# Graph attention with relation biases: a batch's loads in smaller pieces, each waiting for an instruction of its own

## The chip, the cores and the metric

The kernel runs on one core of a Trainium2 chip. The metric is the device time of one execution in microseconds. Before the change the median of three runs is 593.66 us (593.51 to 594.92).

## What is computed

For 16 batches of 512 nodes with 512 features: a linear layer over the node and a condition vector, two attentions (one for each direction of the adjacency) of 16 heads over the first 20 nodes as keys and values, a ReLU, and the residual. Cut to what matters (B = 16, N = 512, F = 512, 11 relation labels, H = 16 heads of 32):

```python
q_exp = where(row_zero[..., None], 0.0, q[:, None, :])
self_feat = concatenate([v, q_exp], -1) @ W_self.T + b_self
output = self_feat
for d in range(2):
    A = (adj if d == 0 else swapaxes(adj, 1, 2))[:, :, :20, :]
    bias = A @ w_bias + b_bias
    qh = self_feat @ Wq[d].T + bq[d];  kh = self_feat[:, :20] @ Wk[d].T + bk[d]
    aff = where(A.sum(-1) > 0, einsum(qh, kh) / sqrt(32), NEG) + bias
    w = softmax(aff, -1)
    output += einsum(w @ self_feat[:, :20], Wout[d]) + bout[d]
return v + relu(output)
```

`row_zero` marks nodes whose features sum to 0.

## The kernel before

**Setup.** The first 100 us or so load the weights, and work out for all batches what depends on the first 20 nodes alone: the keys folded with the query weights (`g_d` in DRAM, 1216 KB a batch), the biases of the scores (`cq_d`, 20 KB for each of four copies) and the values folded with the output weights, in blocks (`bd_d`, 128 KB a batch).

**The loop.** Then a loop runs over the 16 batches b, and within it over four tiles of 128 nodes, `nt` = 0 to 3. The order of the work is written out by hand: every engine runs its instructions in the order of the program text, and so does SyncE (SP), which issues nearly all DMA transfers. A transfer whose operand or whose `behind` instruction isn't done stops SP, and all later transfers with it.

Each tile does the scores (`scores`, 128 matmuls on TensorE into `ps_s`), adds biases and mask, subtracts the maximum (`weigh`, VectorE), takes the exponential (`expo`, ScalarE), sums and divides (`normal`: sum and reciprocal on VectorE, product on GpSimd) and transposes (`turn`, VectorE). It is a pipeline: a tile's `normal` and `turn` run in the next tile's stage, and the product with the values (`attend`, 48 matmuls, line 426) for batch b - 1 runs in stage `nt` = 2 of batch b, with `finish` (the sum with `self_feat` on VectorE, the ReLU on ScalarE), `residual` (GpSimd) and `store` behind it. Between them the stages make the next batch's `self_feat` on TensorE by a scheme with seven products instead of eight (`product`, `x_sum` on GpSimd, `partial` and `joined` on VectorE), its masks and label biases (`mask_mul` on ScalarE, `mask_count`, `mask_sum`, `mask_spread`, `full_add`), and the row sums (`row_sum` on ScalarE, `row_mask`).

**The loads of a batch**, in SP's order over one period, with their size and what each waits for (the `ins` argument of `load_...`, by way of `behind`):

- `nt` = 0: the features transposed, `load_x(b + 1)`, two halves of 512 KB, behind the exponential of the tile before and behind `partial`; `row_mask` writes 2 KB of flags; `load_adj(b + 1, 0)`, 440 KB, behind `mask_sum`
- `nt` = 1: `load_nz` (256 KB, the flags on all partitions) behind an exponential; `load_cq` (4 x 20 KB); `load_adj(b + 1, 1)`, 440 KB, behind `normal`
- `nt` = 2: the features by rows, `load_xn(b + 2, 0)` and `(b + 2, 1)`, 512 KB each, behind the first sum and the first ReLU of `finish`; `load_keys(b + 1)`, first half, 608 KB, behind an exponential
- `nt` = 3: two stores of the output, 256 KB each; the second half of the keys behind `mask_sum`; a third store; `load_values(b)` (`vd`, 4 x 32 KB, one buffer); the fourth store at the start of the next `nt` = 0

Buffers: three of `x` and of `adj`, two of `xn` and of the keys `g`, one of `vd`. `residual` puts its output on a list, and `store()` issues what is on it: at the start of each stage and once in `nt` = 3.

Of the kernel before, what the change touches and what calls it, by code (L numbers as in the profile page):

```python
# [18 lines left out]
def gat_kernel(  # L19
# [87 lines left out]
    def load_xn(b, h, ins=None):  # L107
        t = xns[b, h] = load.tile([P, 2, F], F32, tag="xn", name=f"xn{b}_{h}")
        behind(nc.sync.dma_start(t, xn[b].rearrange("(p j) f -> p j f", j=4)[:, 2 * h : 2 * h + 2]), ins)

    def load_adj(b, h, ins=None):
        t = adjs[b, h] = load.tile([P, 2, S * L], I32, tag="adj", name=f"adj{b}_{h}", bufs=3)
        a = adj[b, h * 2 * P : (h + 1) * 2 * P].rearrange("(t p) d m l -> p t (d m l)", p=P)
        behind(nc.sync.dma_start(t, a), ins)

    def load_cq(b):
        cqs[b] = load.tile([P, HL, S], F32, tag="cq", name=f"cq{b}")
        for a in range(HL):
            nc.sync.dma_start(
                cqs[b][bass.ts(a, R)].rearrange("p h m -> p (h m)"),  # L120
                cq_d[b : b + 1, bass.ts(a, HL)].rearrange("b h d m -> b (h d m)").partition_broadcast(R),
            )
# [9 lines left out]
    def load_values(b):  # L132

        vds[b] = gp.tile([P, HL, 2, DH], F32, tag="vd", name=f"vd{b}", bufs=1)
        for c in range(C):
            nc.sync.dma_start(
                vds[b][bass.ts(c, 32)].rearrange("p e i g -> p (e i g)"), bd_d[c, b].rearrange("r e i g -> r (e i g)")
            )
# [96 lines left out]
    def x_sum(b, n):  # L235

        t = sums[b, n] = xsum.tile([P, 2, HN], F32, tag=f"t{n}", name=f"t{b}_{n}")
        one, two = {
            1: lambda: (x_block(b, 0, 1), x_block(b, 0, 0)),
            2: lambda: (x_block(b, 1, 1), sums[b, 1]),  # L240
            3: lambda: (x_block(b, 1, 1), x_block(b, 0, 1)),
            4: lambda: (x_block(b, 1, 0), sums[b, 2]),
        }[n]()
        nc.gpsimd.tensor_sub(t, one, two)  # L244
# [49 lines left out]
    def joined(b, n, key, f, l):  # L294

        nc.vector.tensor_add(
            block(b, f, l), parts[b, key][:, : 2 * HN].rearrange("p (i n) -> p i n", i=2), us.pop((b, n))
        )
# [37 lines left out]
    def full_add(b, nt):  # L336
        f = fulls[b, nt] = msk.tile([P, H * S], F32, tag="full", name=f"full{b}_{nt}").rearrange(
            "p (g h m) -> p g h m", g=HL, m=S
        )
        shape = [P, HL, HL, S]  # L340
        nc.gpsimd.tensor_add(  # L341
            f, cqs[b].unsqueeze(1).to_broadcast(shape),
            adds[b, nt // 2][:, nt % 2].unsqueeze(2).to_broadcast(shape),
        )
# [19 lines left out]
    def weigh(b, nt, ps, between=None):  # L364
# [10 lines left out]
        nc.vector.tensor_sub(s, f, mx.unsqueeze(3).to_broadcast(full))  # L375
# [28 lines left out]
    def normal(b, nt, s):  # L404
        sm = soft.tile([P, 2, H], F32, tag="sm", name=f"sm{b}_{nt}")
        nc.vector.tensor_reduce(sm, s, AX.X, ALU.add)  # L406
        nc.vector.reciprocal(sm, sm)  # L407
# [24 lines left out]
    def finish(b, o, banks):  # L432

        for c in range(C):
            add = nc.vector.tensor_add(o[:, c], banks[c], sfs[b][:, c])  # L435
            if c == 0:
                done["add"] = add
        for c in range(C):
            relu = nc.scalar.activation(o[:, c], o[:, c], AF.Relu, bias=bo[:, c : c + 1])  # L439
            if c == 0:  # L440
                done["relu"] = relu
# [327 lines left out]
    with tc.manual_schedule():  # L769
# [11 lines left out]
        for b in range(B):  # L781
# [7 lines left out]
            for nt in range(NT):  # L789
# [22 lines left out]
                if nt == 0:  # L812
# [4 lines left out]
                    else:  # L817
# [6 lines left out]
                        if more:  # L824
                            load_x(b + 1, range(2), done["exp"])
                            load_x(b + 1, range(2, C), done["partial"])
# [21 lines left out]
                    if more:  # L848
                        x_sum(b + 1, 1)
                    else:  # L850
# [32 lines left out]
                if nt == 2:  # L883
# [4 lines left out]
                    if b > 0:  # L888
# [16 lines left out]
                    if b > 0 and more:  # L905
                        load_keys(b + 1, range(2), done["exp"])
                    if more:
                        full_add(b, NT - 1)
                    if b > 0:
                        for c in (0, 1):  # L910
                            residual(b - 1, c, o)

                if nt == 3 and more:
# [4 lines left out]
                    x_sum(b + 1, 4)  # L918
                    if b + 2 < B:
# [5 lines left out]
                    if b > 0:  # L925
                        load_keys(b + 1, range(2, C), done["masks"])
# [119 lines left out]
```

## Time and profile before

| | us |
|---|---|
| median of three runs | 593.66 |
| profiled execution, its time | 593.27 |
| its span, first to last instruction | 591.5 |
| TensorE (PE) busy with matmuls | 578.7 |
| VectorE (DVE) busy | 492.3 |
| ScalarE (ACT) busy | 395.6 |
| GpSimd (POOL) busy | 384.2 |
| mean DMA rate over the span | 210 GB/s |

A row of the costliest groups names the line, engine and operation, what is written from what, shapes and count; then busy time, mean duration in ns, and the idle time of the engine just before, with what ended it. PE is the matmul, PEld the loading of its weights, which overlaps it, SPq the queue of SyncE. "issue" stands for time in which an engine waited for nothing that the profile shows. In the list of DMA queues, q1 carries the transfers that the kernel issues from SyncE, and q8 and q14 are marked "instruction". A DMA row gives the size of one transfer and the time from its issue to its landing.

### The profile page before, as it was taken

The page shows a single profiled execution, that of the slowest core. Times are in us where ns is not written, and L with a number is a line of the kernel's source. Part 1 is how long each engine was busy: PE and PEld are TensorE (multiplying, and loading weights), DVE is VectorE, ACT ScalarE, POOL GpSimd, SP SyncE. Part 2 cuts the span into 40 slices and gives each one's busy share as a digit, 9 for nine tenths or more (in the row PEclk, how much of TensorE's full clock was granted, in tenths as well). Part 3 has the DMA queues.
Part 4 walks back from the last instruction along what each step waited for, and adds up shares of the span by engine and source line. Part 5 has one row for each costly group of instructions (what it writes and reads, how often), then busy time and mean ns, then how long its engine had stood idle before and what let it go on. Part 6 is the DMA issues. An engine that isn't in the chain of part 4 may idle for free.

```text
span 591.5 us, 30038 instructions
## 1 busy us (share of the span) xinstructions
PE 578.7 (98%) x13180; PEld 439.7 (74%) x13180; DVE 492.3 (83%) x785; ACT 395.6 (67%) x1162; POOL 384.2 (65%) x351
## 2 busy tenths in 40 slices
PE   8999999999999999999999999999999999999994
PEld 6654547888978687787878787788787878787882
DVE  0495565889898888999999999888989898989896
ACT  1234644587877677768686868677787877777661
POOL 2315663638677675758686777675858677776774
PEclk9999999999999999999999999999999999999997
DMA  8998999857848485767676766757585748582503
GB/s 294 385 406 299 332 376 329 257 126 199 223 154 229 155 236 148 206 168 209 184 208 163 223 173 202 171 181 208 164 217 170 216 149 232 158 238 85 167 13 142
DMA packets 98129, 124.10 MB, mean 210 GB/s; under 512 B 19952, under 2 KB 70160, under 8 KB 95952
## 3 DMA queue, kind: packets, MB, share of 16 engines
q1 hardware_dynamic: 96752, 120.31, 67.1%
q8 instruction: 103, 1.69, 1.2%
q0 software_dynamic: 672, 1.36, 1.0%
q10 hardware_dynamic: 576, 0.53, 0.3%
q14 instruction: 26, 0.21, 0.1%
HBM read 82.30 MB, written 40.24 MB: 207 GB/s over the span
## 4 chain that ended last, share of the span: by engine, by line
PE 94%; DVE 3%; DMA 1%; issue 1%; ACT 0%; POOL 0%; SPq 0%; DVEq 0%; POOLq 0%; ACTq 0%
PE ps_s L353 44%; PE ps_a L279 17%; PE ps_c L279 8%; PE ps_o L426 6%; PE ps_d L279 4%; PE ps_v L644 3%; PE ps_k L581 3%; PE ps_sf L202 2%; DMA ws_q<-in_wsT 1%; PE ps_kv L532 1%; DVE o L435 0%; PE ps_nz L186 0%; DVE wt L415 0%; DVE ps_s L371 0%; DVE sm L406 0%
## 5 line engine op out<-in xcount | busy, mean ns | idle before, releaser
L353 PEld LDWEIGHTS ps_s<-g,sf 128*32 128x32 f32 x8192 | 264.0, 110 | 19.8 <-issue 12.2
L353 PE MATMUL ps_s<-g,sf 128*32 128x152 f32 x8192 | 277.3, 293 | 0.5 <-ACT st L684 0.5
L334 ACT COPY both<-add 32x80 f32<-32x80 f32 x512 | 130.9, 256 | 54.8 <-DVE add L325 49.0
L408 POOL TENSOR_TENSOR s<-s,sm 128x640 f32<-128x640 f32 x63 | 80.3, 1275 | 98.0 <-DVE sm L407 98.0
L341 POOL TENSOR_TENSOR full<-cq,both 128x640 f32<-128x640 f32 x64 | 100.1, 1565 | 30.3 <-issue 24.3
L314 ACT ACTIVATE prod<-adj,wb_sb 128x80 f32<-128x80 int32 x330 | 112.5, 432 | 0.0
L380 ACT ACTIVATE s<-s 128x640 f32<-128x640 f32 x63 | 46.5, 738 | 69.4 <-DVE s L375 69.0
L444 POOL TENSOR_TENSOR o<-o,x 128x512 f32<-128x512 f32 x60 | 75.9, 1285 | 0.0
L367 DVE TENSOR_TENSOR full<-ps_s,full 128x608 f32<-128x608 f32 x63 | 49.1, 779 | 32.1 <-PE ps_s L353 26.6
L406 DVE TENSOR_REDUCE sm<-s 128x32 f32<-128x640 f32 x63 | 50.9, 808 | 8.8 <-ACT s L380 8.6
L279 PE MATMUL ps_a<-t,ws_s 128*32 128x246 f32 x960 | 55.5, 370 | 0.0
L371 DVE TENSOR_REDUCE ps_s<-full 128x32 f32<-128x640 f32 x63 | 52.2, 828 | 2.2
L415 DVE STREAM_TRANSPOSE wt<-s 128x640 f32<-128x640 f32 x63 | 52.8, 839 | 0.1
L375 DVE TENSOR_TENSOR s<-full,ps_s 128x640 f32<-128x640 f32 x63 | 51.6, 818 | 1.1
L426 PE MATMUL ps_o<-wt,vd 32*32 32x512 f32 (+5 forms) x816 | 40.8, 581 | 3.7 <-DVE wt L400 2.0
L279 PEld LDWEIGHTS ps_a<-t,ws_s 128*32 128x32 f32 x960 | 32.2, 110 | 15.5
L325 DVE TENSOR_REDUCE add<-prod 128x80 f32<-128x960 f32 x32 | 36.8, 1150 | 6.3 <-ACT prod L314 4.4
L244 POOL TENSOR_TENSOR t<-x 128x492 f32<-128x492 f32 x30 | 34.4, 1148 | 10.1 <-DVE full L367 5.2
L439 ACT ACTIVATE o<-o,bo 128x512 f32<-128x512 f32 x60 | 38.2, 708 | 0.6 <-POOL biased L881 0.6
L435 DVE TENSOR_TENSOR o<-ps_o,sf 128x512 f32<-128x512 f32 x60 | 36.8, 672 | 1.0 <-PE ps_o L426 1.0
L286 DVE SCALAR_TENSOR_TENSOR u<-nz,qw,ps_a 128x246 f32<-128x246 f32 x90 | 36.6, 449 | 0.0
L244 POOL TENSOR_TENSOR t<-x,t 128x492 f32<-128x492 f32 x30 | 34.4, 1147 | 1.2
(238 smaller groups left out, 722.7 us busy)
## 6 DMA issues: line engine op xcount, KB each, us to landing
g_d<-st SPq DMA_DIRECT2D x16, 1064.0 KB, 5.9
g<-g_d SPq DMA_DIRECT2D x28, 608.0 KB, 5.2
out_T<-o SPq DMA_DIRECT2D x60, 256.0 KB, 4.7
xn<-in_xn SPq DMA_DIRECT2D x28, 512.0 KB, 3.6
x<-in_xT SPq DMA_DIRECT2D x28, 512.0 KB, 4.3
adj<-in_adj SPq DMA_DIRECT2D x32, 440.0 KB, 5.0
nz<-nz_d SPq DMA_DIRECT2D x14, 256.0 KB, 4.0
wk<-in_wkT SPq DMA_DIRECT2D x2, 1024.0 KB, 8.0
```

The source lines that it names most:

```text
L244: nc.gpsimd.tensor_sub(t, one, two)
L279: nc.tensor.matmul(to, lhs, x[:, k], start=start, stop=stop, skip_group_check=n != 2)
L314: nc.scalar.activation(p[:, :, l], a[:, :, l], AF.Identity, scale=wb_sb[:, l : l + 1])
L334: nc.scalar.copy(adds[b, h][bass.ts(a, R), :, g], add[r].rearrange("p (t m) -> p t m", t=2))
L341: nc.gpsimd.tensor_add(f, cqs[b].unsqueeze(1).to_broadcast(shape), adds[b, nt // 2][:, nt % 2].unsqueeze(2).to_broadcast(shape),)
L353: nc.tensor.matmul(bank[bass.ts(a, R), bass.ts(j, WD // HL)], sfs[b][:, k, bass.ds(nt * P + (2 * g + j) * R, R)], keys[:, k, a], start=(k ...
L371: nc.vector.tensor_reduce(mx, f, AX.X, ALU.max)
L375: nc.vector.tensor_sub(s, f, mx.unsqueeze(3).to_broadcast(full))
L408: done["normal"] = nc.gpsimd.tensor_mul(s, s, sm.unsqueeze(3).to_broadcast(full))
L415: nc.vector.transpose(wts[b][:, nt], s.rearrange("p a h m -> p (a h m)"))
L426: nc.tensor.matmul(banks[a][bass.ds(at // 2 * DH, n * DH)].rearrange("p (t n) -> p t n", n=32), vd[r, bass.ds(at * DH, n * DH)], wt[r, :, ...
L444: nc.gpsimd.tensor_add(o[:, c], o[:, c], xs[b][:, c])
```

## The change

No compute instruction is added, removed or moved; each engine but SyncE keeps its order. On SyncE:

- `load_x`: four pieces of 256 KB instead of two of 512. Pieces 0 and 1 move into the end of `nt` = 3 of the batch before, after the stores, behind the subtraction of `weigh` and the exponential; pieces 2 and 3 go in `nt` = 0 behind the sum and the product of `normal`.
- `load_adj`: four pieces of 220 KB instead of two of 440. Each half's first piece waits as the half did; its second waits for an `x_sum`.
- `load_nz` waits for `weigh` instead of the exponential behind it, and `load_cq` for that exponential.
- `load_xn`: four pieces of 256 KB, behind an `x_sum` in `nt` = 1, the second and fourth sum of `finish`, and the sum of `normal`.
- `load_keys`: four pieces of 304 KB, behind `normal` and `full_add` in `nt` = 2, `x_sum` and `normal` in `nt` = 3.
- `load_values` of batch b - 1 moves from the end of `nt` = 3 of batch b - 1's period into `nt` = 0 of the next, after `row_mask` and ahead of `load_adj`, behind `joined`.
- Each output is stored right after its own `residual`.
- The first batches (b = 0, in part 1) keep their whole loads where there is no earlier stage to put them in.

SyncE's program grows from some 22 to some 30 transfers a period.

```diff
-    def load_adj(b, h, ins=None):
-        t = adjs[b, h] = load.tile([P, 2, S * L], I32, tag="adj", name=f"adj{b}_{h}", bufs=3)
+    def load_adj(b, h, ins=None, ts=slice(0, 2)):
+        if ts.start == 0:
+            adjs[b, h] = load.tile([P, 2, S * L], I32, tag="adj", name=f"adj{b}_{h}", bufs=3)
         a = adj[b, h * 2 * P : (h + 1) * 2 * P].rearrange("(t p) d m l -> p t (d m l)", p=P)
-        behind(nc.sync.dma_start(t, a), ins)
+        behind(nc.sync.dma_start(adjs[b, h][:, ts], a[:, ts]), ins)
...
                         if more:
-                            load_x(b + 1, range(2), done["exp"])
-                            load_x(b + 1, range(2, C), done["partial"])
+                            load_x(b + 1, range(2, 3), done["sum"])
+                            load_x(b + 1, range(3, C), done["normal"])
...
                         product(b, 3)
+                        if b > 1:
+                            load_values(b - 1, done["joined"])
                         mask_sum(b, 1)
                         if more:
-                            load_adj(b + 1, 0, done["masks"])
+                            load_adj(b + 1, 0, done["masks"], slice(0, 1))
...
                     if more:
                         x_sum(b + 1, 1)
+                        if b > 0:
+                            load_adj(b + 1, 0, done["xsum"], slice(1, 2))
...
                     if b > 0 and more:
-                        load_nz(b + 1, done["exp"])
-                        load_cq(b + 1)
+                        load_nz(b + 1, done["weigh"])
+                        load_cq(b + 1, done["exp"])
                     normal(*prev)
                     if b > 0 and more:
-                        load_adj(b + 1, 1, done["normal"])
+                        load_adj(b + 1, 1, done["normal"], slice(0, 1))
...
                         x_sum(b + 1, 2)
+                        if b > 0:
+                            load_adj(b + 1, 1, done["xsum"], slice(1, 2))
                         x_sum(b + 1, 3)
+                        if 0 < b < B - 2:
+                            load_xn(b + 2, 0, done["xsum"], slice(0, 1))
...
                         if b + 2 < B:
-                            load_xn(b + 2, 0, done["add"])
-                            load_xn(b + 2, 1, done["relu"])
+                            load_xn(b + 2, 0, done["add", 1], slice(1, 2))
+                            load_xn(b + 2, 1, done["add", 3], slice(0, 1))
                     normal(*prev)
+                    if 0 < b < B - 2:
+                        load_xn(b + 2, 1, done["sum"], slice(1, 2))
+                    if b > 0 and more:
+                        load_keys(b + 1, range(1), done["normal"])
...
                     turn(*prev)
-                    if b > 0 and more:
-                        load_keys(b + 1, range(2), done["exp"])
                     if more:
                         full_add(b, NT - 1)
+                        if b > 0:
+                            load_keys(b + 1, range(1, 2), done["full"])
                     if b > 0:
                         for c in (0, 1):
                             residual(b - 1, c, o)
+                            store()
...
                     x_sum(b + 1, 4)
+                    if b > 0:
+                        load_keys(b + 1, range(2, 3), done["xsum"])
...
                     if b > 0:
-                        load_keys(b + 1, range(2, C), done["masks"])
+                        load_keys(b + 1, range(3, C), done["normal"])
...
                     if b > 0:
-                        residual(b - 1, 2, o)
-                        store()
-                        load_values(b)
-                        residual(b - 1, 3, o)
+                        for c in (2, 3):
+                            residual(b - 1, c, o)
+                            store()
+                    if b + 2 < B:
+                        load_x(b + 2, range(1), done["weigh"])
+                        load_x(b + 2, range(1, 2), done["exp"])
```

More of the change, by code (lines that the diff above doesn't have):

```diff
@@ L243, in x_sum @@
         }[n]()
-        nc.gpsimd.tensor_sub(t, one, two)
+        done["xsum"] = nc.gpsimd.tensor_sub(t, one, two)
     def product(b, n):
@@ L294, in joined @@
     def joined(b, n, key, f, l):
-        nc.vector.tensor_add(
+        done["joined"] = nc.vector.tensor_add(
             block(b, f, l), parts[b, key][:, : 2 * HN].rearrange("p (i n) -> p i n", i=2), us.pop((b, n))
@@ L340, in full_add @@
         shape = [P, HL, HL, S]
-        nc.gpsimd.tensor_add(
+        done["full"] = nc.gpsimd.tensor_add(
             f, cqs[b].unsqueeze(1).to_broadcast(shape),
@@ L374, in weigh @@
         s = soft.tile(full, F32, tag="s", name=f"s{b}_{nt}", bufs=3)
-        nc.vector.tensor_sub(s, f, mx.unsqueeze(3).to_broadcast(full))
+        done["weigh"] = nc.vector.tensor_sub(s, f, mx.unsqueeze(3).to_broadcast(full))
         return s
@@ L406, in normal @@
         nc.vector.tensor_reduce(sm, s, AX.X, ALU.add)
-        nc.vector.reciprocal(sm, sm)
+        done["sum"] = nc.vector.reciprocal(sm, sm)
         done["normal"] = nc.gpsimd.tensor_mul(s, s, sm.unsqueeze(3).to_broadcast(full))
```

28 lines of the change are left out of this document (13 added, 15 removed).

## The prediction

> **What bounds the kernel now.** I read the page first: busy shares, the chain that ended last, the DMA queues.
>
> ```profile
> span 591.5 us, 30038 instructions
> PE 578.7 (98%) x13180; PEld 439.7 (74%) x13180; DVE 492.3 (83%) x785; ACT 395.6 (67%) x1162; POOL 384.2 (65%) x351
> q8 instruction: 103, 1.69, 1.2%
> PE 94%; DVE 3%; DMA 1%; issue 1%; ACT 0%; POOL 0%; SPq 0%; DVEq 0%; POOLq 0%; ACTq 0%
> L353 PE MATMUL ps_s<-g,sf 128*32 128x152 f32 x8192 | 277.3, 293 | 0.5 <-ACT st L684 0.5
> ```
>
> TensorE is busy for 98% and is 94% of the chain. The change touches loads and stores alone, so it can only win what TensorE loses, and the question is where that is. The kernel repeats one period per batch; its clearest mark is the attention product (L426, 48 matmuls). Busy time by stretch, from one such mark to the next (columns: length, busy time of PE, PEld, DVE, ACT, POOL, granted clock, DMA share, GB/s; the first row is all 14 periods):
>
> ```profile
> 133.53:566.24 432.71, 431.31 (x10981) 342.15 (x10977) 391.06 (x602) 327.33 (x985) 308.17 (x267) 1.00 0.66 185
> 164.05:194.95 30.90, 30.90 (x788) 24.38 (x785) 28.01 (x43) 23.50 (x71) 22.13 (x20) 1.00 0.66 191
> 194.95:226.85 31.90, 31.51 (x789) 24.34 (x785) 28.12 (x43) 23.50 (x71) 22.05 (x20) 1.00 0.65 184
> 226.85:258.90 32.05, 31.59 (x785) 24.41 (x785) 28.14 (x43) 23.46 (x71) 21.91 (x20) 1.00 0.64 181
> 258.90:289.38 30.48, 30.48 (x789) 24.15 (x785) 27.83 (x43) 23.53 (x71) 21.87 (x20) 1.00 0.69 193
> 381.01:413.01 32.00, 31.45 (x789) 24.28 (x785) 28.13 (x43) 23.50 (x71) 22.12 (x20) 1.00 0.65 184
> 413.01:444.15 31.14, 31.14 (x788) 24.31 (x784) 28.01 (x43) 23.50 (x71) 21.99 (x20) 1.00 0.69 189
> ```
>
> A clean period is 30.48 us at full clock. Fourteen would be 426.72; they take 432.71, so 5.99 us are lost in all. The five long ones lose 0.42, 1.42, 1.57, 1.52 and 0.66, together 5.59. What happens there shows in the order of time of the weight loads, two bad attention products whole, a good one, and the first row of two more bad ones:
>
> ```profile
> 194.95 0.21 PEld L426 LDWEIGHTS ps_o<-wt,vd 32*32 32x32 f32 x25 [0.24 <-issue]
> 196.45 0.15 PEld L426 LDWEIGHTS ps_o<-wt,vd 32*32 32x32 f32 x7 [1.29 <-issue]
> 226.84 0.14 PEld L426 LDWEIGHTS ps_o<-wt,vd 32*32 32x32 f32 x5 [0.24 <-issue]
> 228.36 0.34 PEld L426 LDWEIGHTS ps_o<-wt,vd 32*32 32x32 f32 x27 [1.38 <-issue]
> 258.90 0.25 PEld L426 LDWEIGHTS ps_o<-wt,vd 32*32 32x32 f32 x32 [0.24 <-issue]
> 381.01 0.21 PEld L426 LDWEIGHTS ps_o<-wt,vd 32*32 32x32 f32 x27 [0.24 <-issue]
> 413.00 0.15 PEld L426 LDWEIGHTS ps_o<-wt,vd 32*32 32x32 f32 x6 [0.24 <-issue]
> ```
>
> The stall comes after 25, 5, 27 or 6 loads, and where its end is shown it ends on "issue": no semaphore that the profile shows. So neither data nor a buffer is late. The instructions themselves are: q8 has 103 packets of 1.69 MB, 16 KB each, and 26,360 matmuls and weight loads by 103 are 256, so one packet brings 256 instructions of TensorE. These packets run on the same DMA engines as the data. Here is the DMA view of the stretches just before and just after 193.9, with the issue of the adj load among them:
>
> ```profile
> GB/s 351 334 334 304 253 235 202 201 137 71 17 90 103 45 45 77 103 33 31 77 74 32 1 14 0 0 0 72 187 216 330 330 345 330 460 302 244 144 101 72
> q1 hardware_dynamic: 584, 0.77, 69.7%
> issues: line engine op xcount, KB each, median us to landing
> adj<-in_adj SPq DMA_DIRECT2D x1, 440.0 KB, 5.1
> ...
> q8 instruction: 1, 0.02, 5.1%
> ...
> L114 SPq DMA_DIRECT2D adj<-in_adj x1: 368/368/368, 189.4 to 189.4; - x1
> ```
>
> From 189.0 to 193.9 there is no q8 row; in 193.9 to 195.1 there is one. The adj load (440 KB) was issued at 189.4 and landed 5.1 later, at 194.5: the instruction packet got its turn only when that load was draining, at 193.9 or just after, and TensorE went on at 196.45, 2.55 later. The load is slow at first (in slices of 0.12 us, some 100 GB/s or less from 190.1 to 192.4), then runs at 330. So the loss is this: **a block of instructions, asked for while a large load stands ahead of it in the DMA engines, comes too late.** At 128 score matmuls in 4.33 us (277.3 x 128 / 8192), a block lasts some 4 us, so it is asked for about that long before it is needed; that, and that it waits for everything issued before it, is my reading and not a row.
>
> The Trainium skill ("Runtime: NRT & Kernel Launch", Instruction fetch mechanics) says that engines refill in 16 KiB blocks of 256 instructions, and that crossing a block is mostly hidden. By that rule there is nothing to win, which is the first rival below; the trace agrees on the block (256), and in the five long periods not on the hiding (1.29 and 1.38 idle).
>
> **The change part by part.** No compute instruction is added, removed or moved. What changes is SP's queue. I lay it over one clean period whose attention product starts at 319.85, with the ends of the instructions that the new loads wait for.
>
> ```profile
> 307.47 0.88 SPq L136 DMA_DIRECT2D vd<-bd_d  x2
> 309.54 2.30 SPq L105 DMA_DIRECT2D x<-in_xT  x2
> 309.81 4.32 PE L353 MATMUL ps_s<-g,sf 128*32 128x152 f32 x128
> 310.90 1.28 POOL L408 TENSOR_TENSOR s<-s,sm 128x640 f32<-128x640 f32 x1 [0.45 <-DVE sm L407]
> 312.32 0.66 DVE L296 TENSOR_TENSOR sf<-ps_c,u 128x492 f32<-128x492 f32 x1
> 314.45 0.37 SPq L114 DMA_DIRECT2D adj<-in_adj  x1
> 314.65 1.05 POOL L244 TENSOR_TENSOR t<-x 128x492 f32<-128x492 f32 x1
> 319.85 2.24 PE L426 MATMUL ps_o<-wt,vd 32*32 32x512 f32 x48
> 323.93 4.10 SPq L109 DMA_DIRECT2D xn<-in_xn  x2
> 326.45 0.35 DVE L407 RECIPROCAL sm<-sm 128x32 f32<-128x32 f32 x1
> 334.08 1.28 POOL L408 TENSOR_TENSOR s<-s,sm 128x640 f32<-128x640 f32 x1
> 334.95 0.38 SPq L130 DMA_DIRECT2D g<-g_d  x1
> ```
>
> *The adj pieces, the term that counts.* The four vd loads now stand ahead of adj: they wait for the join (L296) that ends at 312.98 and take 0.44 each, to 314.8. So the first half (220 KB) issues at 314.8, 5.05 before the attention product, where 440 KB went at 5.40 before; the second half waits for the x sum that ends at 315.70, 4.15 before. A block that is needed early in the attention product was asked for early. In the periods lost to a stall after five or six loads (1.57 and 0.66) I take it as asked for before 5.05 ahead, so it now stands behind x and vd alone and is in time: 2.2 won. In the other three (1.42, 1.52, 0.42) it stands behind the first half: 220 KB less at 330 GB/s is 0.67 sooner, the issue is 0.35 later, so 0.3 each, 0.9 won. Sum 3.1. The bounds: all 5.99 won if no block comes late any more; nothing won if the second half is ahead of it too; worse than nothing under the second rival.
>
> *The other loads*, for their effect on blocks: x goes in four pieces where 1 MB went in two loads, keys in four of 304 KB, xn in four of 256 KB, so that what stands ahead of a block is about half. Outside the long periods only 5.99 - 5.59 = 0.40 is lost; I count nothing for it.
>
> *Data that might now be late.* x pieces 3 and 4 wait for the sum and the normalisation, the latter ending at 312.18, 0.3 after the issuing of today's second load is over (311.84); the x sum and the product that read them come after 319.85. The last keys piece waits for the normalisation that ends at 335.36, 0.4 after today's 334.95; the second half of the next scores reads it at 309.81 + 30.48 + 2.1 = 342.4, 7 us on. The last xn piece goes at 326.80, before the end of issuing today (328.03). All cost nothing.
>
> *vd* is moved furthest: from before 308.4 to 312.98, the last of four issuing at 314.3, behind the last store, all of x and nz_d; TensorE reads it at 319.85. All landings of vd in the steady periods (least, median, most), with its issue times in ns in the row above:
>
> ```profile
> L136 SPq DMA_DIRECT2D vd<-bd_d x56: 380/419/1392, 150.7 to 554.3; - x56
> ...
> DMA to landing us min/median/max: 2.6/4.0/5.5
> ```
>
> At the median the last lands at 318.3, at the most at 319.8, just in time. Only the longest issue (1.39, 1.0 more) and the longest landing together would make TensorE wait, 0.9 in such a period; in all 14 it would be 13, in one or two 1 to 2. I take 0, by the median. *SP* issues about 8 more transfers a period at 0.4, 3 us. It is in order, so behind each wait stand all later loads: behind vd's wait for the join stand adj, nz and cq, read only by the next stage on ACT, DVE and POOL, after 319.85. The instructions waited for end in the order of the queue, so no wait adds to another. *Stores* follow their own residual; no engine waits for a store.
>
> Sum against the profiled run: 593.27 - 3.1 = 590.2. The median of the three runs is 593.66, 0.4 higher; I go to **590.6**.
>
> **The rivals.** (1) *The packet waits as long as before*: both halves and nz are ahead of it, or the 5.6 us are lost to whichever load is ahead. For: the halves go 0.9 apart, and a slow start stays slow. Against: two of the five losses belong to early requests. Between 0 and 1.7 won: 592 to 594, say 593.4. The Trainium skill ("DMA: Bandwidth & Descriptors", Queues, rings and completion order) would have it here: engines take turns between queues packet by packet, so a backlog on q1 would hardly delay q8 and cutting it up would win nothing; that the packet came only as adj drained speaks against. (2) *Slower: the second half of adj has a slow start of its own.* Its place is 4.15 ahead of the attention product. The first half drains 193.9 - 189.4 - 0.67 = 3.8 after issue, 1.25 ahead; another 2.3 slow and 0.67 of data end 1.7 after the start, and TensorE goes on 2.55 later, at 4.3 instead of 1.5 (196.45 for 194.95). Three such periods lose 2.8 more, 8.4, less the 2.2 won: 599.5. It decides from about 1 us of slow start (3 x 1.0 against 3.1 won). Against it: today's second adj load, just behind the first in memory, landed so:
>
> ```profile
> DMA to landing us min/median/max: 3.5/3.5/3.5
> ```
>
> (issued at 195.9), 1.6 less than the first, so about 0.7 of a slow start at the most. (3) *More won*: every late block gone, 587.7.
>
> **How the numbers follow.** A difference under 0.3%, 1.8 us, cannot be told from none here. Forecast 0.53 (588.5 to 591.8), more won 0.06, rival 1 0.23, rival 2 and lesser delays of its kind 0.18 (595.5 to 600). Faster 0.59, same 0.23, slower 0.18. The range 588.0 to 596.0 holds the forecast, rival 1 and the mild part of rival 2; the forecast's own is 588.5 to 591.8.
>
> **What would show it.** Right: periods of 30.5 between attention products with at most two or three over 31, the "issue" idle before L426 in the middle of the product mostly gone, adj landings of 220 KB about 3 to 4 us, vd landed before each product. Wrong: as many periods near 32 as before (rival 1); an adj second half that lands over 4.5 us after issue and stalls above 2 us (rival 2); PE waiting for DMA vd at L426; DVE or POOL waiting for x, g or adj.

## The result, and the profile after

The changed kernel takes 588.80 us (median of six runs, 587.81 to 589.27), the kernel before 593.59 (six runs, 591.39 to 595.43): the ratio is 0.9909, 95% interval 0.9886 to 0.9931. So it is faster by about 0.9%, 4.8 us, in the direction of the forecast, and its median is 1.8 us under the forecast 590.6. On another chip the same two kernels later gave 588.08 and 591.40, ratio 0.9945 (0.9917 to 0.9974).

The profiled execution took 589.14 us, with a span of 587.3. From its page come busy times, the shares of the chain, the group of the scores and the queue of instruction packets.

```profile
span 587.3 us, 30302 instructions
PE 575.0 (98%) x13180; PEld 436.8 (74%) x13180; DVE 491.2 (84%) x785; ACT 395.5 (67%) x1162; POOL 384.3 (65%) x351
q8 instruction: 104, 1.70, 1.2%
PE 94%; DVE 3%; DMA 1%; issue 1%; ACT 0%; POOL 0%; SPq 0%; DVEq 0%; POOLq 0%; ACTq 0%
L356 PE MATMUL ps_s<-g,sf 128*32 128x152 f32 x8192 | 276.7, 293 | 0.5 <-ACT st L683 0.5
```

The page alone tells little: TensorE does the same 13,180 matmuls at the same price and is the bound as before. The difference is in the stretches, from one attention product (now L429) to the next. The first row is again all 14 periods; then come the three longest and, from 286.08, a clean one.

```profile
132.06:561.14 429.08, 428.51 (x10981) 339.57 (x10977) 390.38 (x602) 327.23 (x985) 308.25 (x267) 1.00 0.65 188
132.06:163.50 31.44, 30.87 (x789) 24.29 (x785) 28.01 (x43) 23.74 (x71) 22.94 (x21) 1.00 0.74 216
193.97:224.90 30.93, 30.93 (x789) 24.51 (x785) 28.00 (x43) 23.51 (x71) 22.10 (x20) 1.00 0.67 192
286.08:316.55 30.47, 30.47 (x788) 24.21 (x785) 27.84 (x43) 23.50 (x71) 22.03 (x20) 1.00 0.66 186
377.50:408.76 31.26, 31.26 (x788) 24.44 (x785) 28.01 (x43) 23.50 (x71) 22.17 (x20) 1.00 0.65 192
```

The clean period is unchanged (30.47), the 14 take 429.08 where they took 432.71: 3.63 of the 4.13 us between the two profiled executions (593.27 and 589.14). Of the rest, 1.47 lies ahead of the first product (it begins at 133.53 and 132.06; over all runs here between 132.06 and 136.73), and 0.97 goes the other way after the last. No period is near 32 any more. The weight loads of the worst product that is left, in order of time:

```profile
377.50 0.15 PEld L429 LDWEIGHTS ps_o<-wt,vd 32*32 32x32 f32 x6 [0.24 <-issue]
378.14 0.43 PEld L429 LDWEIGHTS ps_o<-wt,vd 32*32 32x32 f32 x26 [0.49 <-issue]
379.41 0.23 PEld L429 LDWEIGHTS ps_o<-wt,vd 32*64 32x64 f32 x16 [0.84 <-issue]
```

One stall of 0.49 after six loads stands where before had 1.29, 1.38 and their like, and it is not of their kind: here TensorE waits for data. Its product is made in groups of 32 partitions, and each of the four `vd` loads brings one group. These are SP's issues ahead of this product, the landings of the four `vd` loads, and a wait that TensorE's sequencer, which issues its instructions, has in this product:

```profile
370.27 1.35 SPq L174 DMA_DIRECT2D nz_d<-nz  x1
371.73 1.76 SPq L139 DMA_DIRECT2D vd<-bd_d  x4
...
DMA to landing us min/median/max: 3.8/3.9/5.0
...
L429 PEldq EVENT_SEMAPHORE  x1: 51/51/51, 378.1 to 378.1; - x1
```

The fourth `vd` load was issued at 373.07 and took 5.0: it landed at 378.03, 0.53 after the product had begun. The sequencer's wait for its semaphore ended at 378.11, and the next weight load started at 378.14. The row says "issue" because the wait stands on an instruction of the sequencer. In the product at 193.97 the third and fourth `vd` load landed 0.04 and 0.22 after its begin, and the load of weights that needs the fourth started 0.30 later than in a clean product. In both periods the issue of `nz_d` ahead of `vd` took 1.35 or 1.44 us, where the clean period from 286.08 has 0.38. A block of instructions was late in the product at 377.50 as well: after 27 loads there is another pause of 0.17, so without the wait for `vd` not all of the time would have been won.

The view of waits sums the idle time for the loads of weights between 140 and 565 us. First the kernel before, then the changed one (columns: what waited for what, us in total, times, longest):

```profile
PEld ps_o L426 <- issue: 19.0, 31, 1.5
PEld ps_s L353 <- issue: 10.6, 13, 0.8
```
```profile
PEld ps_o L429 <- issue: 15.6, 29, 0.8
PEld ps_s L356 <- issue: 11.4, 14, 0.8
PEld ps_c L282 <- issue: 1.0, 1, 1.0
```

Each product has two regular waits, 0.24 ahead of its first load and 0.84 ahead of its last 16 (both in the rows above), 1.08 in all. The stretch holds 13 products of the kernel before (the next begins at 566.24) and 14 of the changed one, so 14.0 and 15.1 us are the floor. Above it stood 5.0 us in five waits before, and now 0.5 in one, the wait for `vd`. The row of `ps_c` is the long period 132.06:163.50: a new stall in the stage work, not in a product.

The smaller loads land sooner. The DMA issues of the page (count, KB each, median us to landing), before and after:

```profile
g<-g_d SPq DMA_DIRECT2D x28, 608.0 KB, 5.2
...
x<-in_xT SPq DMA_DIRECT2D x28, 512.0 KB, 4.3
adj<-in_adj SPq DMA_DIRECT2D x32, 440.0 KB, 5.0
```
```profile
g<-g_d SPq DMA_DIRECT2D x56, 304.0 KB, 3.6
...
x<-in_xT SPq DMA_DIRECT2D x56, 256.0 KB, 3.3
...
adj<-in_adj SPq DMA_DIRECT2D x56, 220.0 KB, 3.3
```

So far most looks as forecast, but for the waits for `vd`. That the stalls went because adj was halved is, however, only a reading yet.

### The profile page after: what moved, and what is told of

Its sections match the earlier page's. It is cut to its first block, busy times and chain, and to the rows that moved or that the text cites. A ratio compares the mean times of both kernels' runs of the same rounds, so it can differ in the third digit from the quotient of the medians.

```text
span 587.3 us, 30302 instructions
## 1 busy us (share of the span) xinstructions
PE 575.0 (98%) x13180; PEld 436.8 (74%) x13180; DVE 491.2 (84%) x785; ACT 395.5 (67%) x1162; POOL 384.3 (65%) x351
## 4 chain that ended last, share of the span: by engine, by line
PE 94%; DVE 3%; DMA 1%; issue 1%; ACT 0%; POOL 0%; SPq 0%; DVEq 0%; POOLq 0%; ACTq 0%
PE ps_s L356 44%; PE ps_a L282 17%; PE ps_c L282 9%; PE ps_o L429 6%; PE ps_d L282 4%; PE ps_v L643 3%; PE ps_k L580 3%; PE ps_sf L205 2%; DMA ws_q<-in_wsT 1%; PE ps_kv L531 1%; DVE o L438 0%; PE ps_nz L189 0%; DVE wt L418 0%; DVE ps_s L374 0%; DVE sm L409 0%
## 5 line engine op out<-in xcount | busy, mean ns | idle before, releaser
L429 PE MATMUL ps_o<-wt,vd 32*32 32x512 f32 (+5 forms) x816 | 37.8, 578 | 2.3 <-DVE wt L403 2.0
```

Of the source, the lines that this page charges most:

```text
L429: nc.tensor.matmul(banks[a][bass.ds(at // 2 * DH, n * DH)].rearrange("p (t n) -> p t n", n=32), vd[r, bass.ds(at * DH, n * DH)], wt[r, :, ...
```

## The experiments

Each kernel stands beside the kernel before on the same chip. Times are medians; "lost" is the length of the 14 periods of the profiled execution less the clean 426.66 (14 x 30.476).

| kernel | us | before, same chip | ratio (95%) | 14 periods | lost |
|---|---|---|---|---|---|
| before (first profile) | 593.59 | | | 432.71 | 6.0 |
| changed kernel | 588.80 | 593.59 | 0.9909 (0.9886 to 0.9931) | 429.08 | 2.4 |
| adj in pieces only | 592.14 | 592.86 | 0.9991 (0.9961 to 1.0021) | 430.14 | 3.5 |
| changed, adj whole | 587.30 | 592.86 | 0.9905 (0.9886 to 0.9925) | 428.02 | 1.4 |
| changed, vd at its old place | 589.54 | 592.86 | 0.9943 (0.9923 to 0.9964) | 427.87 | 1.2 |
| before, 16 more matmuls at the start | 594.49 (one run) | 592.86 | | 431.42 | 4.8 |
| pieces on the old waits | 590.25 | 592.60 | 0.9961 (0.9945 to 0.9977) | 430.89 | 4.2 |
| x only | 591.20 | 592.60 | 0.9979 (0.9966 to 0.9992) | 430.64 | 4.0 |
| vd only | 590.45 | 592.60 | 0.9967 (0.9949 to 0.9984) | 430.04 | 3.4 |
| first adj load moved away | 590.11 | 592.60 | 0.9976 (0.9956 to 0.9995) | 430.82 | 4.2 |
| vd and x | 590.73 | 591.40 | 0.9985 (0.9963 to 1.0006) | 431.51 | 4.9 |
| changed, adj whole, a spare load | 588.07 | 591.40 | 0.9943 (0.9922 to 0.9964) | 427.14 | 0.5 |
| changed, adj whole, again | 587.73 | 591.40 | 0.9928 (0.9903 to 0.9953) | 426.76 | 0.1 |
| changed kernel, again | 588.08 | 591.40 | 0.9945 (0.9917 to 0.9974) | 426.88 | 0.2 |

One profile is one execution, and the kernel before alone spreads over 589.8 to 596.5 us; so the medians decide on time, and a profile only on where a loss lies. The kernel before was profiled once, on the first chip; what its loop loses on the other chips is not known.

**Is it the blocks of instructions?** Eight more warming matmuls in the setup, with nothing else touched. Each counts as two, so 16 weight loads and 16 matmuls more are in TensorE's stream, and every 256th instruction falls 16 loads earlier in the loop.

```diff
-            for _ in range(7):
+            for _ in range(15):
                 nc.tensor.matmul(warm[:, :P], ones, ones, start=True, stop=True)
```

> The kernel before, with 8 more warm-up matmuls on TensorE ahead of the first load's landing: 16 more pairs of weight load and matmul, 32 instructions, so every block of 256 begins 16 pairs earlier in each later stage. Theory: the stalls in the attention products that came after 25, 27, 5 and 6 weight loads come after 9 and 11, and in the other two batches they leave the product (they would fall 11 and 10 pairs ahead of it, into the scores). Rival (a data or buffer wait): they stay after 25, 27, 5 and 6. Time within 1 us of before either way.

The weight loads of two products in order of time:

```profile
198.44 0.15 PEld L426 LDWEIGHTS ps_o<-wt,vd 32*32 32x32 f32 x9 [0.24 <-issue]
199.57 0.21 PEld L426 LDWEIGHTS ps_o<-wt,vd 32*32 32x32 f32 x23 [0.97 <-issue]
...
382.61 0.16 PEld L426 LDWEIGHTS ps_o<-wt,vd 32*32 32x32 f32 x11 [0.24 <-issue]
384.00 0.20 PEld L426 LDWEIGHTS ps_o<-wt,vd 32*32 32x32 f32 x21 [1.24 <-issue]
```

Where the stalls of these two batches stood after 25 and 27 loads, they now stand after 9 and 11: earlier by 16, exactly the loads that were added. In two more products the place fits too: a stall of 0.68 after 30 loads where before had 0.26 after 46, and, as expected, none where before had one after 5 and after 6. The time, 594.49, is 1.6 above the median of before, not within 1, but it is a single run, and before itself reached 596.5 on this chip. No data and no buffer moved, so the stall belongs to a place in the stream of instructions. This step is shown.

The packet records of the kernel before tell what TensorE waits for there. In all five products with a stall it goes on 1.4 to 1.5 us after the end of a packet of q8 (these start at 163.28, 194.00, 225.97, 380.21 and 411.43). The five packets took 0.88 to 0.98 us, the median of all being 0.97. So they ran no slower than others, they began late.

**Was it adj in pieces?** First adj in four pieces alone, all else as before:

```diff
-                            load_adj(b + 1, 0, done["masks"])
+                            load_adj(b + 1, 0, done["masks"], slice(0, 1))
...
+                        if b > 0:
+                            load_adj(b + 1, 0, done["xsum"], slice(1, 2))
...
-                        load_adj(b + 1, 1, done["normal"])
+                        load_adj(b + 1, 1, done["normal"], slice(0, 1))
...
+                        if b > 0:
+                            load_adj(b + 1, 1, done["xsum"], slice(1, 2))
```

> The kernel before, with adj alone cut into four pieces of 220 KB; all other loads as before. Theory of the prediction (a block of instructions waits for the adj load ahead of it): a block asked for after the first half and before the second waits 0.67 us less, in all five long periods, so 2.5 to 3.3 us are won: 590 to 591. Rival (all loads' backlog counts, adj is only one of them): under 1.5 us won, 592 to 593.5.

The stalls stay at their places and are shorter (rows of the second part of three products):

```profile
194.55 0.15 PEld L427 LDWEIGHTS ps_o<-wt,vd 32*32 32x32 f32 x7 [0.57 <-issue]
...
225.37 0.34 PEld L427 LDWEIGHTS ps_o<-wt,vd 32*32 32x32 f32 x27 [0.34 <-issue]
...
379.21 0.14 PEld L427 LDWEIGHTS ps_o<-wt,vd 32*32 32x32 f32 x5 [0.63 <-issue]
```

In this execution the 14 periods are 2.6 us shorter, near the 3.1 of the prediction's sum, although three new stalls (0.62, 0.35 and 0.76) stand in the stage work. But the median is 0.7 us below that of before, and the interval holds no change. Then the reverse, the changed kernel with adj whole, as two loads on their old waits:

```diff
-                            load_adj(b + 1, 0, done["masks"], slice(0, 1))
+                            load_adj(b + 1, 0, done["masks"])
...
-                        if b > 0:
-                            load_adj(b + 1, 0, done["xsum"], slice(1, 2))
...
-                        load_adj(b + 1, 1, done["normal"], slice(0, 1))
+                        load_adj(b + 1, 1, done["normal"])
...
-                        if b > 0:
-                            load_adj(b + 1, 1, done["xsum"], slice(1, 2))
```

> The changed kernel, with adj in two loads of 440 KB again, on their old waits; vd stays ahead of the first. Theory: 440 KB stand 5.05 us ahead of the attention product; the early blocks escape (2.2 us), the late ones wait 0.35 longer (1.0 us), so most of the gain is lost: 591.5 to 593. Rival (all loads' backlog): nearly all of the gain stays, 588.5 to 590.

The theory's 591.5 to 593 didn't come; the kernel is as fast as the changed one. No product has a stall inside it; the longest of those that make up the 1.4 us lost is 0.56, in the scores. It was run once more on another chip, beside the changed kernel:

> The changed kernel with adj in two whole loads once more, on the same chip and beside the changed kernel itself. If cutting adj wins nothing in the company of the other edits: the same time as the changed kernel within 0.2%. If it costs (two more issues a period and its second piece issued 0.5 to 0.8 later): 0.5 to 1.5 us faster than the changed kernel. By the prediction's own step it would be 2 to 3 us slower.

> The changed kernel itself, unedited, beside the others of this call: 588 to 589.5, ratio to the kernel before 0.990 to 0.993. Every theory expects the same; it is the yardstick for the other three.

All 14 periods, the kernel with adj whole first, then the changed kernel:

```profile
132.07:558.83 426.76, 426.76 (x10980) 338.77 (x10977) 389.69 (x602) 327.30 (x985) 308.58 (x267) 1.00 0.65 188
```
```profile
133.10:559.98 426.88, 426.88 (x10981) 339.75 (x10977) 389.79 (x602) 327.21 (x985) 307.62 (x266) 1.00 0.66 188
```

Both are within 0.2 us of 14 clean periods. The medians, 587.73 and 588.08, lie 0.35 apart, less than either spreads. In the company of the other edits, cutting adj wins nothing; on neither chip was it 2 to 3 us that adj whole gave back.

**Was it vd?** The changed kernel with vd at its old place, behind the third store:

```diff
-                        if b > 1:
-                            load_values(b - 1, done["joined"])
...
+                        load_values(b)
```

> The changed kernel, with the four vd loads back at the end of stage 3, behind the third store. The adj halves then go 5.4 and 4.15 us ahead of the attention product, instead of close together behind vd. If vd ahead of adj is what saves the early blocks, 1 to 2 us are lost against the changed kernel: 590 to 591. If vd only pushes the halves together and is the cause of the stalls that are left, under 588.5 and the long periods near 225 and 378 us are gone.

Neither range was met: the median, 589.54, lies between them. The loop is as good (lost 1.2), the ratio 0.9943 lies between the two that the changed kernel itself had (0.9909 and 0.9945), so by time what vd's move adds in the company of the rest can't be told. The profile does tell where: the two products that still lose time (0.77 and 0.27, at 228.33 and 411.96) belong to the two batches whose stalls came after 5 and 6 loads before. So the order matters for the early blocks, as the prediction had it, but without it the rest of the change already shrinks them from 1.57 and 0.66. In the profiled execution the first product began at 136.73, later than in any other profile here, so what this execution is longer lies in the setup. The other way round, vd moved alone in the kernel before:

```diff
                         product(b, 3)
+                        if b > 1:
+                            load_values(b - 1, done["joined"])
...
                         store()
-                        load_values(b)
```

> Only vd is moved, ahead of adj, as in the change; every other load stays whole and in its place. Theory of the prediction's order term (what matters is that adj goes later, behind four more issues, so that requests made early are no longer behind it): at least the two stalls after 5 and 6 loads go, 14 periods of about 430, time 590 to 591.5. Rival A1 (x ahead of everything is what delays): x still stands ahead and vd adds to it, so 431 to 433, time 592 to 594.

Faster by 0.3%, 2.2 us. The stalls after 25 and 27 loads are still there, 0.80 and 0.57 long where they were 1.29 and 1.46. The one after 6 is gone, and of the one after 5 a delay of 0.27 is left, much as the prediction said of the two early ones. Three new stalls (0.39, 0.72 and 0.37) stand in the stage work.

**Was it x?** Four pieces, two of them a stage earlier, and nothing else:

```diff
-                            load_x(b + 1, range(2), done["exp"])
-                            load_x(b + 1, range(2, C), done["partial"])
+                            load_x(b + 1, range(2, 3), done["sum"])
+                            load_x(b + 1, range(3, C), done["normal"])
...
+                    if b + 2 < B:
+                        load_x(b + 2, range(1), done["weigh"])
+                        load_x(b + 2, range(1, 2), done["exp"])
```

> Only the loads of x are changed as in the change (four pieces, two of them moved into the stage before); adj, vd, xn, keys and stores stay as before. Theory A1 (1 MB of x, issued 10 to 8 us ahead of the attention product, is still draining when adj is issued, and the packet stands behind both): with half of x gone earlier the packet starts sooner, the five stalls shrink to under 0.5 each, 14 periods of 428 to 429.5, time 588.5 to 590. Rival A2 (adj alone is what the packet stands behind): 14 periods as before, 431 to 433, time 592 to 594.

Faster by 0.2%, 1.4 us, between the two theories. The profile has the stalls after 25, 5 and 27 loads still (1.67, 0.34 and 0.84). Then vd and x together, the two diffs above in one kernel:

> Both moves of place at once, x as in the change and vd as in the change; adj, xn and keys stay whole. If the parts add up (x alone took 2.0 us off the 14 periods and vd alone 2.7, of 6.0 lost): 14 periods of 428 to 429, time 588.5 to 589.5, and the rest of the change (keys, xn, stores, nz in pieces) is worth 1 to 2 us more. If they win the same stalls twice: about 430, time 590 to 591.

The first expectation fails. The second has the time right in figure only, 590.73: the kernel before takes 591.40 on this chip, and the interval takes in no change. The parts, measured alone on another chip, don't add here. The profile shows stalls at places where before had none, among them one in the scores of the stage ahead of the product, some 4 us behind the issue of adj (the loads of SP, then the loads of weights, each in order of time):

```profile
494.24 0.38 SPq L171 DMA_DIRECT2D nz_d<-nz  x1
494.73 1.77 SPq L136 DMA_DIRECT2D vd<-bd_d  x4
496.59 0.40 SPq L114 DMA_DIRECT2D adj<-in_adj  x1
```
```profile
497.03 2.65 PEld L353 LDWEIGHTS ps_s<-g,sf 128*32 128x32 f32 x77
500.64 1.69 PEld L353 LDWEIGHTS ps_s<-g,sf 128*32 128x32 f32 x50 [0.96 <-issue]
```

From this kernel to the one with adj whole there is only the rest of the change: keys and xn in pieces, each store right behind its own residual, and the waits of nz and cq. On the same chip these lie 3.0 us apart (590.73 and 587.73; 0.9985 with 0.9963 to 1.0006, and 0.9928 with 0.9903 to 0.9953).

**Is it the size alone?** Each load of x, xn, adj and keys in the loop is issued as two, on the same wait and right behind each other. Here is the edit for adj:

```diff
-        behind(nc.sync.dma_start(t, a), ins)
+        for ts in (slice(0, 1), slice(1, 2)):
+            behind(nc.sync.dma_start(t[:, ts], a[:, ts]), ins)
```

> Theory A (what counts is when the bytes are put in the queue, not how large a piece is): the same bytes go out at the same place, each old load as two transfers with no wait between them, so the five stalls of the kernel before stay: 14 periods of about 432 us, time 592 to 594. Theory B (small transfers as such let the instruction packets in): the stalls go or shrink as in the changed kernel, 14 periods of 429 or less, time 588 to 590.

Faster by 0.4%, 2.4 us: theory A is wrong that pieces on the old waits win nothing. The 14 periods of 430.89 lie between the theories. It is half of what the change wins, and the worst stall is still whole:

```profile
195.74 0.20 PEld L433 LDWEIGHTS ps_o<-wt,vd 32*32 32x32 f32 x24 [0.24 <-issue]
197.41 0.15 PEld L433 LDWEIGHTS ps_o<-wt,vd 32*32 32x32 f32 x8 [1.47 <-issue]
```

**Is it adj at this place?** The first adj load, whole, goes out one batch earlier behind xn in the stage of the product:

```diff
-                        if more:
-                            load_adj(b + 1, 0, done["masks"])
...
                             load_xn(b + 2, 1, done["relu"])
+                            load_adj(b + 2, 0, done["relu"])
```

> The kernel before with the first 440 KB load of adj moved, whole, to just behind xn in the stage of the attention product, one batch earlier; nothing else. Theory A2 (adj ahead of the product is the culprit): no load is issued between vd and the product but nz and cq, all five stalls go, 14 periods of 427 to 428.5, time 587.5 to 589.5; if new stalls come up behind xn and adj there, in the scores of the third stage, they are the same thing in a new place and the time falls less. Rival A1 (x): the packets still stand behind 1 MB of x, 430 to 433, time 591 to 594.

No product has a stall any more; A2 is right about the place, and about new stalls elsewhere. But these are not all behind the moved load. The two in the longest period, from 438.86, are one of 0.90 at 454.05, in the scores of `nt` = 3, after xn, the moved adj (issued at 447.10) and half of the keys, and one of 1.03 at 465.13, in `nt` = 0, behind x and the flags, with no adj load left in that stage:

```profile
284.97:315.77 30.80, 30.80 (x789) 24.30 (x785) 27.83 (x43) 23.61 (x71) 22.35 (x20) 1.00 0.65 192
315.77:347.43 31.66, 31.06 (x785) 24.51 (x784) 28.02 (x43) 23.62 (x71) 21.87 (x20) 1.00 0.62 185
438.86:471.30 32.44, 31.12 (x788) 26.62 (x785) 27.92 (x43) 23.51 (x71) 22.20 (x20) 1.00 0.61 182
```

Moving the load moved the loss; the time fell by 2.5 us, half of what the change wins.

**Do the bytes ahead delay the packet?** In the kernel with adj whole, 440 KB more are loaded in every period, right behind the first adj load, into a buffer that nothing reads:

```diff
                             load_adj(b + 1, 0, done["masks"])
+                            spare = extra.tile([P, 2, S * L], I32, tag="spare", name=f"spare{b}")
+                            nc.sync.dma_start(spare, adj[b, : 2 * P].rearrange("(t p) d m l -> p t (d m l)", p=P))
```

> The changed kernel with adj in two whole loads, and one load added a period: another 440 KB of the same adj, right behind the first adj load, into a buffer that nothing reads. It leaves TensorE's work and every order as they are. Theory A (a packet of instructions waits for what was put in the queue ahead of it): a packet asked for between 3.5 and 1 us ahead of the attention product now stands behind 440 KB more, 0.7 to 1.4 later; the stalls inside that product come back in three to six periods, 14 periods of 430 to 433, time 589.5 to 592.5. Rival (queues take turns packet by packet): the instruction packets start as before, 14 periods of 427 to 429, time 587 to 588.5.

```profile
132.11:559.25 427.14, 427.14 (x10981) 344.98 (x10977) 389.79 (x602) 327.36 (x985) 308.21 (x266) 1.00 0.69 203
```

Theory A's 430 to 433 didn't come, so it is wrong for these bytes. The rate rises from 188 to 203 GB/s, the loop loses 0.5, and the median is 0.34 above that without the load, within the spread. The spare reads what the period before has already read, which may make it quicker than a first read; a spare load of fresh bytes wasn't tried.

## Why the prediction was right, and where not

**The bound and the place of the loss: right.** TensorE sets the time, the clean period stays at 30.48, and 3.63 of the 4.13 us between the two profiles are what it no longer loses in the loop. That the stalls before were late blocks of 256 instructions is shown by the experiment with 16 more matmuls. What makes a block late is not: the prediction's answer, the bytes of a load ahead of it, is not borne out (below). The Trainium skill ("Runtime: NRT & Kernel Launch", Instruction fetch mechanics) calls the crossing of a block mostly hidden. In the runs with adj whole and with the changed kernel on the last chip that holds (0.1 and 0.2 us lost in 14 periods); in the kernel before it didn't (6.0).

**The adj term, "Sum 3.1": its size came near the result by chance.** The prediction gave 2.2 to the order (adj behind vd) and 0.9 to the halving. The order is worth about its figure alone: vd alone won 2.2, and the two early stalls went or shrank, though in its profile the late ones shrank too and new ones came. The halving is worth nothing that could be measured: 0.9991 alone, and nothing between 587.73 and 588.08 in company. That 588.80 lies in the forecast's 588.5 to 591.8 is in good part luck: of the two causes summed, one was worth nothing, and loads that were counted as nothing won more.

**"The other loads ... I count nothing for it": this step failed.** It was argued from 0.40 us lost outside the long periods of one execution. With only vd and x moved no gain could be told from none, and the rest of the change, with keys and xn in pieces and the stores moved, then won 3.0. When a load that hinders the blocks is moved or shortened, blocks come at other times and meet other loads: stalls appeared in the scores (vd and x) and at 454 and 465 us (adj moved away). That is a reading of these profiles, not an experiment of its own. A place that costs nothing in one profile is not safe; it was only not met. Whether keys, xn and stores without x and vd would win 3.0 was not tried. That pieces of all four loads on the old waits win 2.4 fits it.

**The price of bytes, "220 KB less at 330 GB/s is 0.67 sooner": not borne out.** 440 KB more ahead of the product cost 0.34 us in the whole kernel. "The load is slow at first" was right as a row, but taken for a property of adj. It belongs to the place: the packets of an adj row are 1,760 bytes; a quick one takes 73 ns, and in the kernel before some take up to 2.7 us. Counted in the trace's packet records from issue to landing, these took over 500 ns, per load (for loads in two pieces, both together):

```
kernel                          first adj load        loads
before                          15.7                  13
before, 16 more matmuls         18.5                  13
x only                          15.2                  13
adj in pieces only              17.3                  13
pieces on the old waits         18.3                  13
changed, vd at its old place    14.6                  13
vd only (vd ahead of adj)        6.5                  13
changed, adj whole               5.4 and 4.4          13 and 13
first adj load moved away        1.1                  13
second adj load, before          3.6                  13
```

The same load, read behind xn a batch earlier, has hardly a slow packet. Right behind the 2 KB of flags it has 14.6 to 18.5, whole or in pieces, with vd between them 4.4 to 6.5. It is tempting to say that these slow packets hold up the instruction packet. The gain of vd alone fits that; the changed kernel with vd at its old place doesn't: it has 14.6 slow packets, and its loop loses 1.2, not 6.0. What makes the packets slow at that place, and what makes the instruction packet begin late, stays open.

**Rival 1** (the packet waits as long) was given 592 to 594 and didn't come. The rule that went with it, from the Trainium skill ("DMA: Bandwidth & Descriptors", Queues, rings and completion order), that engines take turns between queues packet by packet, looks better than in the prediction: the spare load fits it. **Rival 2** (a slow start of the second half) was wrong on the cost: in the changed kernel the second halves ahead of the product landed after 4.2 at the median, 5 of 13 after more than 4.5, but no stall above 2 us came of it. **Rival 3**, every late block gone, is what the loop shows in two profiles on the last chip (0.1 and 0.2 lost); its 587.7 can't be held against them, since the kernel before takes 591.40 there.

**vd, "I take 0, by the median": wrong in the first profile.** vd's landings in the changed kernel (least, median, most) hardly moved from 2.6, 4.0 and 5.5.

```profile
DMA to landing us min/median/max: 1.6/3.8/5.2
```

But SP issued vd later than was worked out in two of 13 periods, a microsecond behind a slow issue of `nz_d`, and there vd landed after the product had begun. TensorE waited 0.30 and 0.60 us, the sign that the prediction named as wrong, "PE waiting for DMA vd at L426". The prediction had allowed "in one or two 1 to 2" and set it aside. In the changed kernel's second profile the latest vd landed 0.69 ahead of its product, and none was waited for.

**The other data and SP: right to cost nothing.** The halves of adj go out nearer the product and to each other than was worked out, since in 7 of 13 periods one issue among those of vd takes over a microsecond. Here is SP over a clean period whose product begins at 316.55:

```profile
310.69 1.97 SPq L139 DMA_DIRECT2D vd<-bd_d  x2
313.06 0.83 SPq L117 DMA_DIRECT2D adj<-in_adj  x2
314.00 0.85 SPq L178 DMA_DIRECT2D nz<-nz_d  x1
```

The halves were issued 3.5 and 3.0 ahead of the product (forecast: 5.05 and 4.15), 0.5 apart; over 13 periods the medians are 4.1 and 3.5. One more sign named in the prediction as a wrong one does appear, GpSimd waiting for adj. The waits of GpSimd between 140 and 565 us, before and after:

```profile
POOL s L408 <- DVE sm L407: 90.3, 41, 3.7
```
```profile
POOL s L411 <- DVE sm L410: 48.8, 30, 4.4
POOL s L411 <- DMA adj<-in_adj: 36.9, 10, 3.7
...
POOL s L411 <- DMA nz<-nz_d: 3.7, 1, 3.7
```

41 waits of 90.3 us before, 41 waits of 89.4 after: the same waits. The product of `normal` doesn't read adj at all; it waits for the sums of VectorE, and the landing of adj merely came last by the profile. The sign was badly chosen.

## What to carry to other kernels

When TensorE is at its bound and still loses time that ends on "issue", count instructions: if the place shifts with matmuls added far ahead of it, it is the refill of the program, and in these runs changes of loads alone made it come in time or late. First make sure that no semaphore wait of the engine's sequencer ends there: the view called a wait for data "issue" as well. Then spread and shorten all loads, and judge by medians over many runs: single parts of this change won 0.1 to 0.3% each, the one pair that was tried didn't add up, and one profile can show a part as worth 2.6 us that the medians don't confirm. A load moved closer to its reader (here vd) needs room for one slow issue ahead of it. The simplest version found, with adj left in two whole loads, is as fast as the full change.

## What was not expected of the hardware

- A load of the same tensor and size behaves by its place: 16 of its packets took over 500 ns at one place and one at another, where a quick one takes 73 ns.
- 440 KB more per period beside the instruction packets, at 203 GB/s instead of 188, cost TensorE nothing that could be told.
- After a late packet of instructions TensorE goes on only 1.4 to 1.5 us after the packet's end (five stalls of the kernel before).
- The loss differs between executions of one kernel: the changed kernel lost 2.4 us of its 14 periods in one profile and 0.2 in another, on another chip.
